# Graph layers on one Trainium2 core: the adjacency for the masks in SBUF in place of PSUM, and seven common PSUM tiles in place of six

## The chip, the core and the metric

The kernel runs on one core of a Trainium2 chip. A core has TensorE (matrix products; PE in the profile, PEld for its weight loads), VectorE (DVE), ScalarE (ACT), GpSimd (POOL) and SyncE (SP, which issues the transfers here), each with an instruction queue of its own. Two on-chip memories matter in this document: SBUF, the working memory, and PSUM, into which TensorE writes its products. The metric is the device time in microseconds (us) of one launch.

## The reference

The input is a batch of 128 graphs of 128 nodes with 256 features each, and one integer adjacency matrix per graph. Two layers follow one another. The first is a graph attention layer: two rounds of attention with a softmax masked by `adj > 0`, a LayerNorm, a feed-forward block with ReLU, a second LayerNorm. The second layer is a transformer layer with eight heads whose attention weights are split by relation. That split is what the change touches:

```python
q = (src @ Wq + bq) ...; k = (src @ Wk + bk) ...          # 8 heads of 32 features
attn = softmax(q k^T / sqrt(dh))
out = 0
for r in range(4):                                        # four relations
    v_r = src @ Wv[r] + bv[r]
    mask = (adj_matrix == r)
    out = out + einsum('bhij,bhjd->bhid', attn * mask, v_r)
x = LayerNorm(src + out @ Wo + bo)
return LayerNorm(x + gelu(x @ W1 + b1) @ W2 + b2)
```

All of it is in 32-bit floats. (The adjacency holds only 0 and 1 here, but all four relations are computed.)

## The kernel before

The graphs are handled in 32 groups of four (`G = 4`). The stages of neighbouring groups (graph attention, first feed-forward, second attention, second feed-forward) are interleaved: a list of times decides in which order the Python code emits the steps of all groups, and TensorE's queue keeps that order. The other engines' queues are ordered when the program is built. Each group takes one turn of a pattern that repeats.

The pools of buffers:

```python
wk = ctx.enter_context(tc.tile_pool(name="wk", bufs=2))                    # SBUF
ps = ctx.enter_context(tc.tile_pool(name="ps", bufs=6, space=PSUM))        # the common tiles "mm"
```

In the second layer's attention, the adjacency of the group is turned from integers to floats once, and then serves 16 products: four graphs by four relations. Each product makes the masked attention weights of all eight heads of one graph (128 x 1024 elements):

```python
adj = ps.tile([P, G, N], F32, name="adj", bufs=1)          # L434
nc.vector.tensor_copy(adj, at)                             # L435, from int32 in SBUF
...
def turned(e):                                             # attention weights, transposed
    eT = wk.tile([P, H, N], F32, name="eT")
    transposed(e, eT, direct, e)                           # VectorE by blocks (L262), then DRAM and back
    return eT

def by_relation(b, eT, ms, parts):
    ab = adj[:, b][:, None, :].to_broadcast([P, H, N])
    for r in parts:
        m = ms[r] = wk.tile([P, H, N], F32, name="m", bufs=R)
        nc.vector.scalar_tensor_tensor(m, ab, r, eT, op0=OP.is_equal, op1=OP.mult)    # L470

def weighted(ms, v):
    po = ps.tile([P, DC, N], F32, name="av", bufs=1)
    ...                                                    # L489: TensorE, 64 products from ms and v
```

The first layer's attention has a similar mask, `cap`, in SBUF:

```python
def gat_weighting(wh, c, cap, direct):
    ...
    nc.vector.scalar_tensor_tensor(e, cap, BIG, e, op0=OP.subtract, op1=OP.min)       # L374
    ...
    nc.gpsimd.tensor_mul(e, e, per_row(s, N))              # L381

def gat_block(direct, tag, g, xt, at):
    cap = wk.tile([P, G, N], F32, name="cap")              # two buffers
    nc.vector.tensor_scalar(cap, at, 0, 2 * BIG, op0=OP.is_gt, op1=OP.mult)           # L387
```

The feed-forward block forms the first product from seven partial products (L307 on TensorE) that are added up partly in PSUM and partly on VectorE. Cut to one unit:

```python
chain, side = (ps.tile([P, 2, T // 2], F32, name="mm") for _ in range(2))
product(chain, 1, True); product(side, 5, True)
nc.scalar.copy(lo[:, :, 0], chain); nc.scalar.copy(hi[:, :, 1], side)
yield
p = ps.tile([P, 2, T // 2], F32, name="mm")
product(chain, 6); product(p, 2, True); product(side, 3)
nc.scalar.copy(lo[:, :, 1], chain)
nc.vector.tensor_add(lo[:, :, 0], lo[:, :, 0], p)          # L321
nc.vector.tensor_add(lo[:, :, 1], lo[:, :, 1], side)       # L322
yield
product(chain, 7)
nc.vector.tensor_add(hi[:, :, 1], hi[:, :, 1], chain)      # L325 reads chain
...
yield
product(chain, 4)                                          # writes chain again
```

The second products are L350, with their sum into the tokens on VectorE at L351. GpSimd works from SBUF to SBUF alone: scale and offset of the LayerNorms (`affine`, L245), the small operations of their statistics (L233 to L237), the division of the softmax (L456 and L381), and the sums of the moving operands (L283 to L286). L239 is the LayerNorm's own scaling on ScalarE, L262 a transposition on VectorE ahead of the trip through DRAM, L478 the bias of the values on VectorE. In the preparation of the weights, L200 to L204 are VectorE operations on weights in SBUF.

Of the kernel before, what the change touches and what calls it, by code (L numbers as in the profile page):

```python
# [12 lines left out]
F32 = mybir.dt.float32  # L13
# [4 lines left out]
PSUM = bass.MemoryType.PSUM  # L18
# [4 lines left out]
P = 128  # L23
G = 4
# [33 lines left out]
def graph_layers(ctx: ExitStack, tc: tile.TileContext, a: dict, out: bass.AP):  # L58
# [10 lines left out]
    NG, N, _, D = x.shape  # L69
# [14 lines left out]
    ld = ctx.enter_context(tc.tile_pool(name="ld", bufs=2))  # L84
    wk = ctx.enter_context(tc.tile_pool(name="wk", bufs=2))
    sm = ctx.enter_context(tc.tile_pool(name="sm", bufs=4))
    ps = ctx.enter_context(tc.tile_pool(name="ps", bufs=6, space=PSUM))
    dr = ctx.enter_context(tc.tile_pool(name="dr", bufs=3, space=bass.MemoryType.DRAM))

    ident = cst.tile([P, P], F32, name="ident")  # L90
# [324 lines left out]
    def attention(y, g, first, direct):  # L415
# [15 lines left out]
            for q in range(2):  # L431
                nc.scalar.activation(kbd[c][:, :, q], p, AF.Identity, scale=own[:, q:q + 1], bias=bk_own[q][:, c:c + 1])

        adj = ps.tile([P, G, N], F32, name="adj", bufs=1)  # L434
        nc.vector.tensor_copy(adj, at)  # L435

        def weights(b):
# [125 lines left out]
    def stage_attention(g):  # L563
        if g == 0:
            folded(wq, bq, "02")
            folded(wkk, bk, "02")
            for q in range(2):
                nc.vector.tensor_scalar(bk_own[q], bk, own[:, q:q + 1], None, op0=OP.mult)
            folded(wv_all, bv, "02", rows=True)
            folded(w1, b1, "11")  # L570
            later["w1"] = weight_sums(w1, "w1")
        x2[g] = yield from attention(x1.pop(g), g, g == 0, g == NG - 1)
# [91 lines left out]
```

## Time and profile before

| what | value |
| --- | --- |
| time, median of 3 | 3208.48 us (3208.29 to 3210.35) |
| span of the profiled launch | 3208.9 us, 55180 instructions |
| TensorE busy | 3124.8 us, 97% |
| VectorE busy | 2019.9 us, 63% |
| ScalarE busy | 1688.2 us, 53% |
| GpSimd busy | 1377.3 us, 43% |
| granted TensorE clock, mean | 0.989 |
| mask products L470 (VectorE) | 512 of 1213 ns, 598.8 us busy |
| affine L245 (GpSimd) | 380 of 128x512, 1276 ns; 256 of 128x256, 738 ns |
| softmax division L456 (GpSimd) | 256 of 1040 ns |
| mask step L374 (VectorE) | 64, 681 to 1192 ns, median 693 |
| cast L435 (VectorE) | 32 of 688 ns |

A share is that of the whole span; what an engine's time is worth is seen only from the waits. In the profile's lists, a line gives the start in us from the span's start, the duration in us, the engine, the line of the kernel, the operation, output and inputs with their shapes, and how often it ran; several like instructions in a row are drawn together. In brackets stands how long the engine sat idle before, and which instruction it waited for. A list of waits gives the engine and line that waited, what released it, and the time in total, how many times, and the longest.

### The profile page before, as it was taken

The numbers are of one execution on the slowest core, as the hardware profiler recorded it, in microseconds if no ns is written. First come the engines' busy times: TensorE is split into PE (matmuls) and PEld (weight loads), VectorE is DVE, ScalarE is ACT, GpSimd is POOL, SyncE is SP. The second block draws the span as 40 slices with busy tenths as digits, with TensorE's granted clock in tenths as the row PEclk, the third lists the DMA queues.
The fourth block names the chain that finished last, engine by engine and source line by source line (L and its number), as shares of the span: only waits on it lengthen the run. The fifth ranks groups of instructions, "written<-read, shape, count | busy, mean of one in ns | idle before, by whom it ended". The sixth has DMA issues, their size and how long they took to land.

```text
span 3208.9 us, 55180 instructions
## 1 busy us (share of the span) xinstructions
PE 3124.8 (97%) x20160; PEld 2377.2 (74%) x20160; DVE 2019.9 (63%) x3654; ACT 1688.2 (53%) x5063; POOL 1377.3 (43%) x1734
## 2 busy tenths in 40 slices
PE   6989999999999999999999999999999999999998
PEld 5756777777777777777777777777777777777666
DVE  3566566666566666576666576666576666576563
ACT  4435555555555555555555555555555555555443
POOL 2324345345345344345344345344345344345342
PEclk8999999999999999999999999999999999999999
DMA  4244454444454444454444454444454444454310
GB/s 156 66 105 96 102 119 102 107 99 100 102 120 104 105 98 101 101 120 104 105 100 98 101 120 104 104 99 99 102 120 104 104 99 99 102 120 92 73 34 14
DMA packets 1156399, 320.82 MB, mean 100 GB/s; under 512 B 902944, under 2 KB 1126688, under 8 KB 1156000
## 3 DMA queue, kind: packets, MB, share of 16 engines
q1 hardware_dynamic: 1156128, 317.29, 43.5%
q8 instruction: 160, 2.62, 0.3%
q14 instruction: 111, 0.91, 0.1%
HBM read 187.58 MB, written 129.62 MB: 99 GB/s over the span
## 4 chain that ended last, share of the span: by engine, by line
PE 58%; DVE 4%; DMA 1%; issue 0%; ACT 0%; POOL 0%; SPq 0%; ACTq 0%; POOLq 0%; DVEq 0%
PE mm L350 18%; PE mm L307 15%; PE mm L477 7%; PE av L489 5%; DVE m L470 3%; PE mm L444 3%; PE mm L527 2%; PE mm L430 2%; PE mm L424 2%; PE mm L392 2%; PE mm L400 1%; PE mm L410 1%; DVE fT L325 0%; DVE fT L322 0%; DMA eT<-zd 0%
## 5 line engine op out<-in xcount | busy, mean ns | idle before, releaser
L470 DVE SCALAR_TENSOR_TENSOR m<-adj,eT 128x1024 f32<-128x1024 f32 x512 | 598.8, 1213 | 242.5 <-DMA eT<-zd 176.9
L245 POOL TENSOR_TENSOR tok<-tok,ln_rows 128x512 f32<-128x512 f32 (+1 forms) x636 | 668.6, 1059 | 42.2 <-PE mm L256 14.8
L456 POOL TENSOR_TENSOR e<-e,s 128x512 f32<-128x512 f32 x256 | 266.1, 1040 | 660.9 <-DVE s L455 648.9
L454 ACT ACTIVATE e<-mm,nm 128x128 f32<-128x128 f32 x1024 | 359.8, 374 | 199.7 <-DVE nm L450 178.0
L477 PE MATMUL mm<-wv,T 128*128 128x512 f32 x1024 | 464.2, 596 | 0.0
L350 PE MATMUL mm<-wf,fT 128*128 128x256 f32 x2048 | 456.9, 381 | 0.0
L350 PE MATMUL mm<-w,fT 128*128 128x256 f32 x2048 | 455.5, 381 | 1.1 <-DVE v L478 1.1
L350 PEld LDWEIGHTS mm<-w,fT 128*128 128x128 f32 x2048 | 386.6, 190 | 75.5 <-issue 23.8
L350 PEld LDWEIGHTS mm<-wf,fT 128*128 128x128 f32 x2048 | 386.4, 190 | 63.3 <-ACT wh L401 8.9
L239 ACT ACTIVATE tok<-tok,nmr,rstd 128x256 f32<-128x256 f32 x512 | 269.2, 594 | 137.7 <-POOL nmr L237 125.1
L477 PEld LDWEIGHTS mm<-wv,T 128*128 128x128 f32 x1024 | 191.5, 190 | 199.6 <-issue 189.3
L351 DVE TENSOR_TENSOR tok<-tok,mm 128x512 f32<-128x512 f32 x128 | 87.8, 686 | 299.4 <-PE mm L350 295.4
L381 POOL TENSOR_TENSOR e<-e,s 128x512 f32<-128x512 f32 x64 | 66.9, 1046 | 475.3 <-DVE s L380 381.1
L489 PE MATMUL av<-m,v 128*32 128x128 f32 x8192 | 256.2, 277 | 8.1 <-DVE v L478 4.2
L489 PEld LDWEIGHTS av<-m,v 128*32 128x32 f32 x8192 | 219.8, 111 | 54.1 <-issue 42.2
L283 POOL TENSOR_TENSOR t<-T 128x256 f32<-128x256 f32 x64 | 46.7, 729 | 483.6 <-DMA T<-zd 483.6
L454 ACT ACTIVATION_READ_ACCUMULATOR e<-mm,nm 128x1 f32 x1024 | 218.8, 214 | 0.0
L450 DVE TENSOR_REDUCE nm<-mm 128x4 f32<-128x512 f32 x256 | 162.9, 676 | 64.0 <-PE mm L444 64.0
L478 DVE TENSOR_TENSOR v<-mm,bv 128x512 f32<-128x512 f32 x256 | 167.5, 684 | 46.9 <-PE mm L477 46.9
L307 PE MATMUL mm<-T,w 128*128 128x256 f32 x768 | 196.5, 385 | 0.2 <-ACT T L260 0.2
L307 PE MATMUL mm<-T,wf 128*128 128x256 f32 x768 | 192.6, 380 | 0.0
L373 ACT ACTIVATE e<-e,wh 128x128 f32<-128x128 f32 x240 | 77.3, 408 | 210.2 <-DMA e<-zsd 210.2
(123 smaller groups left out, 5090.1 us busy)
## 6 DMA issues: line engine op xcount, KB each, us to landing
zd<-e SPq DMA_DIRECT2D x496, 128.0 KB, 3.1
eT<-zd SPq DMA_DIRECT2D x124, 512.0 KB, 4.0
zd<-T SPq DMA_DIRECT2D x364, 128.0 KB, 4.0
T<-zd SPq DMA_DIRECT2D x91, 512.0 KB, 4.0
xt<-in_xT_dram SPq DMA_DIRECT2D x32, 512.0 KB
at<-in_adjT_dram SPq DMA_DIRECT2D x64, 256.0 KB, 6.2
tok<-in_x_dram SPq DMA_DIRECT2D x32, 512.0 KB
out_dram<-tok SPq DMA_DIRECT2D x31, 512.0 KB, 7.5
```

The costliest lines, as they stand in the source:

```text
L239: nc.scalar.activation(y[:, b], y[:, b], AF.Identity, bias=nmr[:, b:b + 1], scale=rstd[:, b:b + 1])
L245: engine.tensor_tensor(y[:, b:b + n], y[:, b:b + n], v[:, None, :].to_broadcast([P, n, D]), op)
L307: nc.tensor.matmul(p[:, i], win[k][:, ts(f0 + i, P)], hs[k], start=first and i == 0, stop=True, skip_group_check=True)
L350: nc.tensor.matmul(p[:, b - b2_], fT[f][:, ts(b, N)], wout[:, f], start=n == 0, stop=n == FC - 1)
L444: nc.tensor.matmul(scores[h][:, c], qT[rows, c, ts(b, N)], kbd[c][rows, b], start=True, stop=True, tile_position=(h * P // 2, 0))
L450: nc.vector.tensor_reduce(nm, p, AX.X, OP.max, negate=True)
L454: nc.scalar.activation(eh[:, q], p[:, q], AF.Exp, bias=nm[:, q:q + 1], accum_out=s[:, q:q + 1])
L456: nc.gpsimd.tensor_mul(eh, eh, per_row(s, N))
L470: nc.vector.scalar_tensor_tensor(m, ab, r, eT, op0=OP.is_equal, op1=OP.mult)
L477: nc.tensor.matmul(p, hT[:, b, f], wv[:, f, r:r + 2], start=f == 0, stop=f == DC - 1)
L478: nc.vector.tensor_add(v[:, r:r + 2].rearrange("p r d -> p (r d)"), p.rearrange("p r d -> p (r d)"), bv[:, r * D:(r + 2) * D])
L489: last = nc.tensor.matmul(po[ts(q, DH), c], v[:, r, c * P + q * DH:c * P + (q + 1) * DH], ms[r][:, q // 2 * HC + c * 2 + q % 2], start=r = ...
```

## The change

The float copy of the adjacency leaves PSUM for SBUF, where it shares the two buffers of `cap`. The tile of PSUM that it leaves free goes to the common pool, which all products use, so that TensorE may be one more tile ahead of the engines that read its results.

```diff
-    ps = ctx.enter_context(tc.tile_pool(name="ps", bufs=6, space=PSUM))
+    ps = ctx.enter_context(tc.tile_pool(name="ps", bufs=7, space=PSUM))
...
-        adj = ps.tile([P, G, N], F32, name="adj", bufs=1)
+        adj = wk.tile([P, G, N], F32, name="adj", tag="cap")
         nc.vector.tensor_copy(adj, at)
```

Nothing else differs: the same instructions with the same shapes run on the same engines.

## The prediction

> **What bounds the kernel now.** I read the page's shares first (TensorE, PE, busy 97% of 3208.9 us; VectorE, DVE, 63%; ScalarE, ACT, 53%; GpSimd, POOL, 43%), then busy time by window, TensorE's waits, the chain that ended last, and the timelines of VectorE and GpSimd. From about 300 to 2880 us the kernel repeats itself: one stall of TensorE comes back at 2052.01 and, five groups later, at 2533.22 us, so a group takes 481.21 / 5 = 96.24 us. One such group:
>
> ```profile
> core 0: us, PE busy (x) PEld busy (x) DVE busy (x) ACT busy (x) POOL busy (x), PEclk, DMA share, GB/s
> 1500.00:1596.20 96.20, 95.63 (x635) 72.93 (x628) 62.48 (x114) 52.60 (x158) 43.23 (x56) 1.00 0.47 106
> ```
>
> TensorE is idle for 0.57 us of it. Its waits, restricted to 300 to 2880 us, are one line, for one reason, once a group:
>
> ```profile
> PE mm L307 <- DVE fT L325: 16.2, 27, 1.1
> ```
>
> The chain of work in that group runs on TensorE everywhere except here, where it passes over VectorE:
>
> ```profile
> 1565.96 0.04 issue
> 1565.99 3.48 DVE m L470 x3
> 1569.47 0.59 DVE fT L322
> 1570.06 0.61 DVE fT L325
> 1570.67 0.14 issue
> 1570.81 1.97 PE mm L307 x8
> ```
>
> Columns are start, duration, what. The reader is to see three mask products (L470), which nobody on TensorE needs at that moment, standing in VectorE's queue ahead of L322 and L325; L325 reads the accumulator that TensorE's next products (L307) will overwrite, so they wait for it. **At this one place in each group VectorE has no slack: what lengthens those masks lengthens the kernel.** The other three sets of masks end 7.9, 9.2 and 12.0 us ahead of the L489 products that read them (masks over at 1509.36, 1536.26, 1583.68; products from 1517.28, 1545.46, 1595.71); the set at this place ends 5.0 us ahead (1569.47 against 1574.44).
>
> **What the Trainium skill says.** "SBUF — State Buffer", section "Who interferes with whom": a VectorE instruction with two SBUF inputs contends with a GpSimd instruction that reads SBUF, while one with at most one SBUF input, outside the two-port modes, does not. The mask product now reads adj from PSUM and eT from SBUF; after the change it reads both from SBUF. The trace agrees on both sides. L470 takes 1190 to 1226 ns in all 512 cases, whatever GpSimd does. L374, the one frequent VectorE product with two SBUF inputs, varies from 681 to 1192 ns:
>
> ```profile
> 1554.24 2.61 POOL L245 TENSOR_TENSOR tok<-tok,ln_rows 128x512 f32<-128x512 f32 x2
> ...
> 1556.22 1.18 DVE L374 SCALAR_TENSOR_TENSOR e<-cap,e 128x512 f32<-128x512 f32 x1
> ...
> 1588.85 0.69 DVE L374 SCALAR_TENSOR_TENSOR e<-cap,e 128x512 f32<-128x512 f32 x1 [4.03 <-ACT e L373]
> ```
>
> The first began 0.63 us ahead of GpSimd's end (1556.85) and took 0.49 us more; the second, with GpSimd idle, took 0.69. Second place, "PSUM — Partial Sum Buffer", section "Specifications (TRN2)": eight banks of 2 KiB per partition. An mm tile, adj (4x128 floats) and av each take one: 6+1+1 before, 7+1 after, both full. Third, "VectorE: DVE Perf Modes", section "Why PSUM operands drop a tier": an fp32 copy with a PSUM operand runs at one element a cycle, SBUF to SBUF at two. The trace agrees: 512 elements from int32 take 688 ns into PSUM (L435) and 412 ns into SBUF (L387). Fourth, "Perfetto Trace Analysis", section "Optimization Strategy" under "Identifying Performance Opportunities": a consistent bubble can mean too few buffers. Here the trace speaks against it: the bubble's releaser is L325, which reads the same accumulator that is written again, and not a tile that would come out of the pool.
>
> **Part by part.** *Seven tiles.* In the steady part nothing waits for a free tile: 0.57 us a group is all there is, and its cause is the dependency above. Matmuls run evenly there (32 products of L350 in 6.91 us of the chain, 216 ns each), so a deeper pool can't speed them either. TensorE's listed waits before 300 us (the largest 5.29 us for POOL L381, 3.92 for masks) and after 2880 us are for data too. I allow -3 us, a choice.
>
> *The cast L435.* 0.69 becomes about 0.41 us, once a group, at a place where TensorE doesn't wait for VectorE: 0.
>
> *The buffer.* adj takes one of the two buffers tagged cap. In a group cap is written at 1521.91 and last read at 1588.85; adj is written at 1536.50, right behind the last mask set of the group before. Two tensors alternate over two buffers, adj having had one all along; all writers and readers are on VectorE, in order. No new wait: 0.
>
> *The masks.* Without contention I leave L470 at 1.21 us: two SBUF inputs cost L374 693 ns in the median, a PSUM and an SBUF input cost L478 684, the same shape. With contention each of the 16 masks of a group pays where a GpSimd read is under way. How the two engines share is seen once in the trace, when weights are prepared around 109 us (between the lines lie others of the two engines):
>
> ```profile
> 108.65 1.24 POOL L245 TENSOR_TENSOR tok<-tok,ln_rows 128x256 f32<-128x256 f32 x1
> ...
> 109.22 1.21 DVE L203 TENSOR_TENSOR w<-w 128x512 f32<-128x512 f32 x1
> ```
>
> A lone 128x256 L245 takes 0.74 us and a VectorE product of 512 elements 0.68; here they take 1.24 and 1.21, each lengthened by about the other's hold, and six L245 stretch over 6.63 us. So they alternate, one instruction each; neither engine is shut out for long. At the place without slack the two queues are:
>
> ```profile
> 1564.10 1.28 POOL L245 TENSOR_TENSOR tok<-tok,ln_rows 128x512 f32<-128x512 f32 x1
> ...
> 1564.86 4.61 DVE L470 SCALAR_TENSOR_TENSOR m<-adj,eT 128x1024 f32<-128x1024 f32 x4
> ...
> 1565.46 0.23 POOL L233 TENSOR_SCALAR rstd<-mv 128x4 f32<-128x4 f32 x1
> 1565.77 0.23 POOL L235 TENSOR_SCALAR nmr<-mv 128x4 f32<-128x4 f32 x1
> 1565.96 0.20 POOL L237 TENSOR_TENSOR nmr<-nmr,rstd 128x4 f32<-128x4 f32 x1
> 1566.11 0.73 POOL L245 TENSOR_TENSOR tok<-tok,ln_rows 128x256 f32<-128x256 f32 x1
> ```
>
> The first mask meets L245 until 1565.38: 0.52 us of overlap, less the 0.14 us that L374's case left free (0.63 - 0.49), is 0.38. With alternation one small operation of 128x4 goes between masks 1 and 2, one between 2 and 3, one between 3 and 4. Each is 0.20 to 0.23 us long[...]; I take 0.1 for each, a choice. Together 0.38 + 0.3 = about 0.7 us, straight onto L325 and TensorE. From 300 to 2880 us there are 27 such places, 30 in the whole list of waits: 30 x 0.7 = **21 us**.
>
> *The other masks.* At 1501.51 the first meets L286, at 1579.95 and 1581.35 they meet L456: 0.5 to 1 us each, on VectorE or on GpSimd, with slacks of 5 us and more: 0 for TensorE. GpSimd loses about 3 us behind the four masks (its L237 at 1565.96 has to let three masks pass), which delays the LayerNorm on ScalarE and the transpose L262 at 1572.37; VectorE then idles 2.20 us before 1575.81 anyway, which takes most of it up.
>
> *Ends.* In the first 300 and the last 330 us TensorE does wait for masks, values and GpSimd (3.92, 1.88, 5.29, 3.29 us at the start; 2.34, 0.85, 2.79 at the end), and longer masks and GpSimd operations land there in part: +6 us, a choice.
>
> Sum: 3208.5 + 21 + 6 - 3 = 3232 us.
>
> **The rivals.** (1) *The contention is hidden.* Then the time stays at 3208, at best a little under it. For it: all averages (VectorE 63%, GpSimd 43%) leave room. Against it: the chain above. (2) *The stall vanishes.* If the order of VectorE's queue comes out differently because the seventh tile or the new costs change the planned order, L325 may come ahead of the masks; 0.57 us x 30 = 17 us would be gained: 3191. Nothing in the profile speaks for or against it, since the order is made when the program is built; TensorE's order is pinned. (3) *GpSimd goes first.* If every waiting GpSimd operation passes ahead of VectorE's next mask, not one each in turn, the four masks pay for nearly all GpSimd work from 1564.86 to 1569.47: about 3.5 us of it reads whole rows; less overheads 2.5 to 3 us a group, 75 to 90 us: about 3290. The head's alternation speaks against it. (4) *VectorE becomes the bound.* With 62.48 us busy a group, all 16 masks delayed by 1 us each would make 78 us of 96: not yet.
>
> **Range and chances.** The middle is the sum, 3232. Rivals 1 and 2 set the low end, 3200; the doubled site cost (1.5 us x 30 = 45) with a second place losing its slack sets the high end, 3275. Faster by over 2% would need 64 us, more than all of TensorE's idle time in the steady part (17 us) and what the ends could yield: 0.01. Slower by over 2% (above 3272.6) is rival 3 or an unlucky order: 0.12. Within 2%: 0.87.
>
> **What would show it.** Right: L470 spread from 1.19 up to about 2.2 us with a mean of 1.35 to 1.6; L245 and L456 longer in the mean; L435 at 0.41; TensorE's wait for L325 up from 0.57 to about 1.3 us a group, and a group of about 97 us. Wrong: L470 still at 1213 ns throughout (no contention), waits for L325 gone (another order), or a new line in TensorE's waits as large as this one (a slack that I called sufficient was not).

## The result and the profile after

The changed kernel takes 3343.48 us (median of 4 runs, 3338.31 to 3349.62) against 3209.41 us for the kernel before (4 runs, 3208.29 to 3210.38): a ratio of 1.0419, 95% interval 1.0395 to 1.0442. It is slower by 134 us; 24 were predicted.

The page after, its busy times and the line of the masks (busy us, then mean ns of one):

```profile
PE 3164.2 (95%) x20160; PEld 2389.9 (72%) x20160; DVE 2128.9 (64%) x3654; ACT 1682.4 (50%) x5063; POOL 1618.9 (49%) x1734
...
L470 DVE SCALAR_TENSOR_TENSOR m<-adj,eT 128x1024 f32<-128x1024 f32 x512 | 717.3, 1438 | 236.4 <-DMA eT<-zd 216.8
```

The reader is to see that both partners of the contention grew: the masks from 1213 to 1438 ns (118 us in all), GpSimd's busy time from 1377.3 to 1618.9 us (242 us), though GpSimd has the same work. One L470 now lasts anything from 1182 to 2310 ns. Neither engine is near its limit, so the averages alone would still allow a kernel of 3209 us. TensorE's waits between 300 and 2880 us don't:

```profile
PE mm L307 <- DVE fT L325: 54.1, 26, 2.4
PE mm L444 <- ACT fT L333: 20.4, 21, 1.1
PE mm L307 <- ACT fT L313: 5.3, 8, 1.6
PE mm L350 <- DVE v L478: 4.5, 8, 1.3
```

Before, only the first of these was there, with 16.2 us. It has more than tripled, and a second wait, for ScalarE, is new. One group of the changed kernel, several engines in one list; lines between those shown are left out, here and in the lists that follow:

```profile
1529.92 5.09 DVE L470 SCALAR_TENSOR_TENSOR m<-adj,eT 128x1024 f32<-128x1024 f32 x3
...
1530.09 3.85 POOL L245 TENSOR_TENSOR tok<-tok,ln_rows 128x512 f32<-128x512 f32 x2
...
1534.02 1.09 POOL L233 TENSOR_SCALAR rstd<-mv 128x4 f32<-128x4 f32 x1
...
1535.62 2.08 ACT L239 ACTIVATE tok<-tok,nmr,rstd 128x256 f32<-128x256 f32 x4 [4.24 <-POOL nmr L237]
1538.09 1.97 PE L307 MATMUL mm<-t,wf 128*128 128x256 f32 x8 [1.87 <-DVE fT L325]
...
1539.77 2.08 ACT L239 ACTIVATE tok<-tok,nmr,rstd 128x256 f32<-128x256 f32 x4 [2.08 <-POOL nmr L237]
1541.75 1.32 ACT L327 ACTIVATE fT<-fT,col 128x512 f32<-128x512 f32 x2
...
1545.44 1.13 PE L444 MATMUL mm<-kbd,T 64*128 64x256 f32 x6 [1.13 <-ACT fT L333]
```

Two things are to be read from it. First, VectorE's queue has another order than before: three masks now stand ahead of the last L321 and a fourth ahead of L322, and beside the three stand two full-width L245. Three masks take 5.09 us (1.70 each, about 1.15 before), two L245 3.85 (1.93 each, 1.28 before). Second, an operation of 128x4 elements, L233, took 1.09 us instead of 0.23. Behind it L237 came late, so ScalarE stood still for 4.24 us, and everything behind L239 in ScalarE's queue, L327 and L333, moved back with it. L333 reads the accumulators that the next products of TensorE overwrite.

Starting each group at the L307 that waits, a group takes 100.24 us in the mean of 26, against 96.27 before. From the starts of each line on TensorE, compared with before, 1.50 us of the 3.97 are lost at L307, 1.33 between L489 and L350 (where L444 waits for L333), 0.35 at other L307 products, where they wait for ScalarE's L313, 0.26 ahead of L350, where it waits for the values L478, and 0.42 in products that last longer, all of them in groups in which the granted clock fell; the last 0.1 is spread. Between 300 and 2880 us it fell to 0.50 seven times, for 3.41 us each, and not once before the change. One of the seven, TensorE alone (start and end, length, busy time and count, granted clock, then the transfers):

```profile
934.88:938.29 3.41, 3.41 (x10) 0.50 0.00 0
```

Added up over the launch: the first such L307 starts 13.5 us later (332.4 against 318.9), 26 groups lose 26 x 3.97 = 103.2, and the end 11.3. Together that is the difference of the two profiled spans, 3337.0 - 3208.9 = 128.1 us.

### The profile page after: what moved, and what is told of

It is laid out like the page before. It is cut to its first block, busy times and chain, and to the rows that moved or that the text cites. A ratio compares the mean times of both kernels' runs of the same rounds, so it can differ in the third digit from the quotient of the medians.

```text
span 3337.0 us, 55148 instructions
## 1 busy us (share of the span) xinstructions
PE 3164.2 (95%) x20160; PEld 2389.9 (72%) x20160; DVE 2128.9 (64%) x3654; ACT 1682.4 (50%) x5063; POOL 1618.9 (49%) x1734
## 5 line engine op out<-in xcount | busy, mean ns | idle before, releaser
L470 DVE SCALAR_TENSOR_TENSOR m<-adj,eT 128x1024 f32<-128x1024 f32 x512 | 717.3, 1438 | 236.4 <-DMA eT<-zd 216.8
L245 POOL TENSOR_TENSOR tok<-tok,ln_rows 128x512 f32<-128x512 f32 (+1 forms) x636 | 737.1, 1168 | 39.0 <-PE mm L256 15.0
L456 POOL TENSOR_TENSOR e<-e,s 128x512 f32<-128x512 f32 x256 | 320.8, 1258 | 624.5 <-DVE s L455 609.9
L350 PE MATMUL mm<-w,fT 128*128 128x256 f32 x2048 | 457.3, 381 | 5.0 <-DVE v L478 4.8
L350 PE MATMUL mm<-wf,fT 128*128 128x256 f32 x2048 | 460.4, 383 | 0.9 <-ACT fT L333 0.9
L350 PEld LDWEIGHTS mm<-w,fT 128*128 128x128 f32 x2048 | 385.3, 190 | 84.4 <-DVE v L478 21.3
L350 PEld LDWEIGHTS mm<-wf,fT 128*128 128x128 f32 x2048 | 388.6, 191 | 65.2 <-ACT wh L401 9.3
L239 ACT ACTIVATE tok<-tok,nmr,rstd 128x256 f32<-128x256 f32 x512 | 265.7, 593 | 270.0 <-POOL nmr L237 258.5
L489 PE MATMUL av<-m,v 128*32 128x128 f32 x8192 | 257.0, 278 | 15.0 <-DVE v L478 10.7
L381 POOL TENSOR_TENSOR e<-e,s 128x512 f32<-128x512 f32 x64 | 67.0, 1046 | 408.6 <-DVE s L380 304.5
L489 PEld LDWEIGHTS av<-m,v 128*32 128x32 f32 x8192 | 220.4, 111 | 60.5 <-issue 41.2
L307 PE MATMUL mm<-T,w 128*128 128x256 f32 x768 | 198.1, 387 | 3.5 <-DVE tok L411 3.2
L307 PE MATMUL mm<-T,wf 128*128 128x256 f32 x768 | 192.6, 380 | 0.0
L444 PE MATMUL mm<-kbd,T 64*128 64x256 f32 x1024 | 162.9, 407 | 20.9 <-ACT fT L333 20.9
L230 DVE BATCH_NORM_STATS2 st<-tok 128x6 f32<-128x256 f32 x512 | 181.1, 409 | 0.5
```

The source lines that it names most:

```text
L230: nc.vector.bn_stats(st, y[:, b])
L239: nc.scalar.activation(y[:, b], y[:, b], AF.Identity, bias=nmr[:, b:b + 1], scale=rstd[:, b:b + 1])
L245: engine.tensor_tensor(y[:, b:b + n], y[:, b:b + n], v[:, None, :].to_broadcast([P, n, D]), op)
L307: nc.tensor.matmul(p[:, i], win[k][:, ts(f0 + i, P)], hs[k], start=first and i == 0, stop=True, skip_group_check=True)
L350: nc.tensor.matmul(p[:, b - b2_], fT[f][:, ts(b, N)], wout[:, f], start=n == 0, stop=n == FC - 1)
L444: nc.tensor.matmul(scores[h][:, c], qT[rows, c, ts(b, N)], kbd[c][rows, b], start=True, stop=True, tile_position=(h * P // 2, 0))
```

## The experiments

**How they are built.** The theory is that adj in SBUF makes masks and GpSimd block one another, and that the loss comes through the waits above. The first rival: the seventh tile led to another planned order of the queues, and the order costs the time. In runs marked "order held", an order recorded from the kernel before (from the changed one in one_input) is imposed on all engines by ordering dependencies between neighbours in a queue. This puts 64 lines ahead of the code, so in their profiles every line number is higher by 64: L371 is L307, L389 L325, L397 L333, L303 L239, L309 L245, L414 L350, L464 L400, L508 L444, L534 L470, L542 L478, L553 L489, L591 L527. Ratios are to the kernel before, with 95% intervals.

### Contention or order: five runs

**six_tiles.** The changed kernel with the common pool as before. Its queues come out in the order of the kernel before, with nothing imposed (VectorE's differs in 36 of 3659 places, near the end).

```diff
-    ps = ctx.enter_context(tc.tile_pool(name="ps", bufs=7, space=PSUM))
+    ps = ctx.enter_context(tc.tile_pool(name="ps", bufs=6, space=PSUM))
```

> Adjacency in SBUF, but six common tiles (one bank of PSUM stays empty). Built so, PE, ACT, GpSimd and SP have their queues in the order of before, and VectorE's differs in 36 of 3659 places. Theory C (the masks' two SBUF inputs collide with GpSimd, and this alone costs the 134 us): about 3340 us, L470 with a mean of 1.40 us or more. Theory O (the seventh tile changes the planned order of the queues, and the new order is what costs; contention costs only what I predicted for it): 3225 to 3245 us. If the two only act together: in between.

Measured: 3354.55 us, 1.0447 (1.0431 to 1.0463). adj in SBUF alone, in the old order, costs all of it and slightly more. Since the order is the old one, this trace can be laid beside the site shown in the prediction:

```profile
1524.80 5.03 DVE L470 SCALAR_TENSOR_TENSOR m<-adj,eT 128x1024 f32<-128x1024 f32 x4
...
1525.42 1.09 POOL L233 TENSOR_SCALAR rstd<-mv 128x4 f32<-128x4 f32 x1
1526.59 1.05 POOL L235 TENSOR_SCALAR nmr<-mv 128x4 f32<-128x4 f32 x1
1527.61 1.14 POOL L237 TENSOR_TENSOR nmr<-nmr,rstd 128x4 f32<-128x4 f32 x1
...
1528.78 2.07 ACT L239 ACTIVATE tok<-tok,nmr,rstd 128x256 f32<-128x256 f32 x4 [3.44 <-POOL nmr L237]
...
1531.16 1.97 PE L307 MATMUL mm<-t,wf 128*128 128x256 f32 x8 [0.99 <-DVE fT L325]
...
1538.35 1.54 ACT L333 ACTIVATE fT<-mm,col 128x256 f32<-128x256 f32 x4
1539.21 1.87 PE L444 MATMUL mm<-kbd,T 64*128 64x256 f32 x8 [2.46 <-ACT fT L333]
```

The four masks take 5.03 us, only 0.42 more than before, and TensorE's wait for L325 grows by the same 0.42, from 0.57 to 0.99. Each small GpSimd operation, however, waits for one whole mask: 1.09, 1.05 and 1.14 us instead of 0.23, 0.23 and 0.20. The first L237 ends 3.95 us after the masks began, against 1.30 before; the second 8.71 against 5.07. So the second block of L239 is 3.6 us late relative to the masks, L327 and L333 behind it as well, and TensorE waits 2.46 us at L444, where it hadn't waited at all. L327 needed L325's sums, which had been there since 1531.62; it started at 1535.52, when L239 was through. The Trainium skill, "TensorE: Matmul & The Clock Gate", section "Architectural detail: the array is 16× 32×32, not 1× 128×128", states that ScalarE's and VectorE's queues are strictly first in, first out; these times agree.

The wait at L444 has a second cost. Windows of the same trace, TensorE alone:

```profile
1336.11:1339.52 3.41, 1.68 (x8) 1.00 0.84 131
1339.52:1342.93 3.41, 3.41 (x9) 0.50 0.36 83
...
1537.49:1540.91 3.42, 1.67 (x8) 1.00 0.84 131
1540.91:1544.32 3.41, 3.41 (x9) 0.50 0.34 74
1544.32:1547.73 3.41, 3.41 (x18) 1.00 0.76 262
```

From 1540.91 us, 1.7 us after the wait, which ended at 1539.21, the granted clock is 0.50 for 3.41 us, and 32 products of L350 take 8.79 us in place of 7.17. About every second group shows it: groups last 101.5 and 99.9 us in turn. The same page of the skill, section "What's actually happening" under its Part 1, states that the clock falls to half after an idle window of about 3.4 us and that the windows run freely. The half rate agrees. The idle time does not: here a wait of 2.46 us was enough, in a stretch of 3.42 us in which TensorE was still busy for 1.67, and the measurement decides. The free running fits: the two low stretches shown begin 201.39 us apart, which is 59 times 3.413 us, and that is also the time of two groups. So in every second group the wait lies in the same place of such a window.

**after_old_order.** Both parts of the change, order held.

```diff
     ps = ... bufs=7 ...; adj = wk.tile(..., tag="cap")
+    # all queues held in the order of the kernel before
```

> The changed kernel (seven tiles, adjacency in SBUF) with all five queues held in the order of before. Theory C: about 3340 us. Theory O: 3225 to 3245 us, and the same as with six tiles, as nothing waited for a free tile in the steady part. A gain of the seventh tile by itself would show as a difference from the six-tile kernel.

Measured: 3366.61 us, 1.0502 (1.0466 to 1.0539). With the old order held the full change is no faster, so its new order isn't what makes it slow. The extra tile shortens the single wait at L444 (46.8 us in 26 waits, 63.9 in six_tiles), but the low clock follows in nearly every group:

```profile
837.65:844.47 6.82, 6.67 (x17) 0.50 0.67 151
...
940.05:946.87 6.82, 6.67 (x17) 0.50 0.69 154
...
1042.45:1049.27 6.82, 6.70 (x17) 0.50 0.46 87
```

These begin 102.40 us apart, 30 times 3.413 us, and that is the time of one such group: each meets the window as the one before did. The mean granted clock of the launch is 0.967 (0.981 in six_tiles, 0.985 in the changed kernel).

**av_common.** Seven common tiles with adj still in PSUM; the tile that this takes is won from the weighted sums instead, which now come from the common pool. VectorE's order becomes nearly that of the changed kernel.

```diff
-        adj = wk.tile([P, G, N], F32, name="adj", tag="cap")
+        adj = ps.tile([P, G, N], F32, name="adj", bufs=1)
...
-            po = ps.tile([P, DC, N], F32, name="av", bufs=1)
+            po = ps.tile([P, DC, N], F32, name="mm")
```

> Seven common tiles with the adjacency left in PSUM: the accumulator av takes its tile from the common pool, which frees a bank. No mask has two SBUF inputs. VectorE's queue is then nearly that of the changed kernel (120 of 3659 places differ from it, 771 from before). Theory C: 3195 to 3215 us, L470 at 1.21 us throughout. Theory O: 3300 us or more, with masks standing between L321, L322 and L325 and a value sum L478 behind the four masks that wait for a transfer.

Measured: 3238.79 us, 1.0092 (1.0076 to 1.0107). All 512 masks take 1185 to 1226 ns. Seven tiles and nearly the new order without contention cost 29 us, over the 3195 to 3215 us expected, of which the shared tile for the sums may have a part: not a pure measurement of the order.

**one_input** and **one_input_old.** Seven tiles; each mask product is replaced by a transposition of eT, of the same shape and with one input in SBUF. The relations are left out of the result, and adj is computed but not read. The first has the changed kernel's order exactly, the second the old one; both orders are held.

```diff
-                nc.vector.scalar_tensor_tensor(m, ab, r, eT, op0=OP.is_equal, op1=OP.mult)
+                nc.vector.transpose(m, eT)
```

> The changed kernel with all queues held exactly in its own order, and each mask product replaced by a block transposition of eT of the same size (128x1024): one SBUF input, no masking, so the relations are left out of the result. The transposition of this size takes 1.23 us where it occurs before. Theory C: about 3210 us, no stretched GpSimd operations. Theory O: still 3300 us or more, as the order is the same. In between: what is left above 3210 is the order's share.

> Seven tiles, masks replaced by block transpositions of the same size (one SBUF input, relations left out), all queues in the order of before. What the new order costs by itself is the difference from the same kernel with the new order (3222 us): if the order costs the 13 us that stood above before, this is 3205 to 3212 us; if the transposition is what costs them, 3220 us.

Measured: 3222.22 us, 1.0038 (1.0024 to 1.0053), and 3208.52 us, 0.9993 (0.9984 to 1.0001). With one SBUF input in place of the masks' two the loss is all but gone, with seven tiles and in either order, and so is the stretching on GpSimd: in one_input every L233 of 128x4 takes 232 to 246 ns, as before (up to 1157 in the changed kernel). Two results follow: contention is the cause of about nine tenths of the loss, and the new order by itself costs 3222.22 - 3208.52 = 13.7 us. The latter lies at the start: one_input's groups are as long as before (96.32 us), but the first of them starts 12.4 us later than in one_input_old, behind this wait, which one_input_old doesn't have:

```profile
248.13 3.45 PE L553 MATMUL av<-m,v 128*32 128x128 f32 x64 [8.64 <-DVE v L542]
```

The changed kernel has it too (7.82 us at 251.24). In the first 200 us TensorE's own order differs too, in 234 places; the prediction took it for pinned, which holds in the steady part only. And the seventh tile alone gains nothing that can be measured without contention: one_input_old equals the kernel before. With contention and the old order it comes out 12 us slower (3366.61 against 3354.55 us), with the lowered clock in more groups.

### Where the contention hurts: seven runs

The theory after six_tiles: late statistics on GpSimd delay L239, and with it L333, because all stand in one queue. If so, moving one of the three engines' instructions must shift the wait. All seven have the order held but for the moves shown; each is made in 28 groups, and xN is a number of instructions. Where nothing else is said there are six common tiles and adj is in SBUF.

**scale_later.**

```diff
 ScalarE
-  L327 x2, L239 x8,           L327 x2, L333 x8
+  L327 x2, L239 x4,           L327 x2, L333 x8, L239 x4
```

> The six-tile kernel with the adjacency in SBUF and all queues in the order of before, but for one move in each group on ScalarE: the four scalings L239 of the second of two LayerNorms in a row stand behind L327 and L333 in place of ahead of them. Theory S (the masks hold GpSimd's small operations L233, L235, L237 up, L237 comes late, L239 blocks ScalarE's queue in front of L333, and L333 is what frees the accumulators that TensorE needs for L444 and L350): the wait of L444 for L333, 2.46 us a group, goes, and with it the lowered clock behind it; about 3215 to 3235 us. Theory M (the masks' own length ahead of L325 is what costs): no change, about 3350 us.

Measured: 3359.21 us, 1.0462 (1.0448 to 1.0477). The gain expected under theory S did not come. L444's wait for L333 is gone, which shows that the place of L239 in the queue caused it; but new waits came (its waits between 300 and 2880 us):

```profile
PE mm L591 <- DVE v L542: 45.7, 25, 2.8
PE av L553 <- DVE v L542: 26.7, 26, 2.2
```

As read from the trace, the later half of L239 delays the transposition of the tokens, its trip through DRAM and a row of scores behind it in the transfer queue; VectorE stands still 6.09 us for these scores, and the values (L542, that is L478) behind them are late. That half of L239 is urgent as well. The lateness must be taken away where it arises.

**two_first.** The kernel before (adj in PSUM), with VectorE's order changed so that two of the four masks let the chain pass. This takes the known 0.57 us wait away.

```diff
 VectorE
-  L470 x4, L322, L325 x2,          L478 x2
+  L470 x2, L322, L325 x2, L470 x2, L478 x2
```

> The kernel before (adjacency in PSUM, six tiles) with the move on VectorE alone: in each group two of the four masks stand behind L322 and L325. If the 0.57 us that TensorE waits for L325 is that queue and nothing else, it vanishes: 28 groups at 0.57 to 0.74 us are 16 to 21 us, so 3188 to 3194 us. If another wait takes its place: 3209.

Measured: 3210.29 us, 0.9999 (0.9991 to 1.0007). The wait for L325 is gone and the time is the same. The list of weight loads, for 28 groups, shows where it went:

```profile
PEld mm L508 <- ACT fT L397: 20.9, 56, 0.4
```

That is 0.75 us a group, at L444 behind ScalarE's L333: **already before the change, two chains ended within about 0.1 us of one another, and the wait at the first hid the second.** TensorE's list of waits showed only the first.

**both_moves.** scale_later and two_first's move together, with adj in SBUF.

```diff
 ScalarE as in scale_later, VectorE as in two_first
```

> As scale_later, and on VectorE two of the four masks of the zero-slack place stand behind L322 and L325 in place of ahead of them. Under theory S the time is that of scale_later less the wait of L307 for L325 (0.99 us a group with six tiles): 3190 to 3215 us, though all masks still have two SBUF inputs. Under theory M: at least 25 us less than scale_later, but still over 3300.

Measured: 3329.41 us, 1.0369 (1.0355 to 1.0383): 30 us better than scale_later. The waits for L542 ahead of L591 (45.4 us) remain, beside 26.9 us of L307 for ScalarE's L313 and 18.6 of L400 for L333.

**six_stats_first.** GpSimd computes both sets of statistics before the affines that stood between them.

```diff
 GpSimd
-  L381, L233, L235, L245, L236, L245, L233, L235, L237, L245, L236, L245 x2, L237
+  L381, L233, L235, L236, L237, L233, L235, L236, L237, L245 x5
```

> Six tiles, adjacency in SBUF, all queues in the order of before but for GpSimd's: in each group the statistics of two LayerNorms (L233, L235, L236, L237, twice) stand ahead of five affine operations L245 in place of among them, and so mostly ahead of the four masks. Theory S2 (the masks make GpSimd's L237 late by about 3 us, and this reaches TensorE over L239, either through L333 and the accumulators or through the transposition L262 and the transfers behind it): 3215 to 3250 us, with no wait for L333 over 0.5 us a group. Rival D (VectorE and GpSimd can't do their common work one after the other in the time of a group, whatever their order): still 3320 us or more.

Measured: 3311.15 us, 1.0311 (1.0292 to 1.0329), 43 us better than six_tiles. The wait at L444 is gone, as it must be if the statistics delay it. But the other one grew, from 0.99 to 2.74 us:

```profile
1511.22 6.78 DVE L534 SCALAR_TENSOR_TENSOR m<-adj,eT 128x1024 f32<-128x1024 f32 x4
...
1512.45 12.12 POOL L309 TENSOR_TENSOR tok<-tok,ln_rows 128x512 f32<-128x512 f32 x8
...
1519.34 1.97 PE L371 MATMUL mm<-t,wf 128*128 128x256 f32 x8 [2.74 <-DVE fT L389]
```

Beside the masks there is now an unbroken row of wide affines. The two engines take turns instruction by instruction here, so now the masks pay in full: 6.78 us for four, where 128x4 operations between them had made it 5.03. The loss is moved from GpSimd's chain to VectorE's, which stands on the same TensorE.

**six_stats_two.** The same, with the VectorE move of two_first.

```diff
 GpSimd as in six_stats_first, VectorE as in two_first
```

> As six_stats_first, and two of the four masks stand behind L322 and L325 on VectorE. Under S2 the wait for L325 goes too: 3190 to 3225 us with all masks from SBUF. Under D: over 3300.

Measured: 3260.64 us, 1.0147 (1.013 to 1.0164), 94 of six_tiles' 145 us recovered. Both waits at this place are gone but for one of 1.0 us, and a third has come: behind the two masks that were moved, the values L478 are late for L400. TensorE's waits between 300 and 2880 us (L464 is L400, L377 L313):

```profile
PE mm L591 <- DVE v L542: 14.5, 22, 2.4
PE mm L464 <- DVE v L542: 11.6, 27, 2.4
PE mm L371 <- ACT fT L377: 10.8, 6, 1.8
```

The largest lies at the mask set of another graph:

```profile
1526.71 3.20 DVE L534 SCALAR_TENSOR_TENSOR m<-adj,eT 128x1024 f32<-128x1024 f32 x2 [0.63 <-DMA eT<-zd]
...
1528.79 1.71 POOL L349 TENSOR_TENSOR T<-T 128x256 f32<-128x256 f32 x1
...
1533.52 0.67 PE L591 MATMUL mm<-wo,oT 128*128 128x256 f32 x2 [1.17 <-DVE v L542]
```

Two masks last 3.20 us beside the sums of moving operands (L349 is L285: 1.71 us, 0.73 before), and the values L542 behind them are late for L591. These links are read from the trace; no run took them away.

**after_stats_first.** GpSimd's move with seven tiles.

```diff
 bufs=7, adj in SBUF; GpSimd as in six_stats_first
```

> The changed kernel (seven tiles, adjacency in SBUF) with the queues in the order of before and GpSimd's statistics first. Under S2: 3215 to 3250 us, within 10 us of the six-tile one; a gain of the seventh tile would show as the difference. Under D: 3320 us or more.

Measured: 3304.27 us, 1.0298 (1.0282 to 1.0314), 62 us better than after_old_order. It agrees with six_stats_first.

**before_stats_two.** Both moves in the kernel before, adj in PSUM.

```diff
 bufs=6, adj in PSUM; GpSimd as in six_stats_first, VectorE as in two_first
```

> The kernel before (adjacency in PSUM, six tiles) with both moves. The earlier run with the VectorE move alone changed nothing, because the wait for L325 became one of 0.7 us for L333, behind L239 and L237. If L237 is what that wait comes from, both are gone: 28 groups at 0.74 us are 21 us, so 3186 to 3194 us. If a third wait of the same size lies behind: 3209.

Measured: 3186.43 us, 0.9927 (0.9914 to 0.9939): **faster than both kernels**, and 24 us ahead of the one before (3210.51 us on the same chip). Its list of TensorE's waits in the steady part is empty and a group takes 95.43 us. two_first's move alone gave nothing; together with the earlier statistics it does, which confirms the second chain. The same eight affines that took 12.12 us in six_stats_first run undisturbed here:

```profile
1556.82 9.32 POOL L309 TENSOR_TENSOR tok<-tok,ln_rows 128x512 f32<-128x512 f32 x8
```

**What the seven runs show together.** With adj in SBUF none of the five came down to what theory S or S2 expected. scale_later and both_moves came out where rival M had put them (about 3350 us, then at least 25 less but over 3300); 3311, 3304 and 3261 us lie between S2 and rival D. The waits went where each move should send them, so the path over L237, L239 and L333 is real; but it is one of several that are about equally tight, and clearing one brings out the next. What contention costs can't be put down to one path.

## Why the prediction was wrong

**The mechanism was right.** adj in SBUF made the masks contend with GpSimd; L470's mean (1438 ns) and the cast L435 (0.42 us) are in the ranges given; the engines alternate one instruction each in the places shown, as read from the head of the launch, and GpSimd doesn't shut VectorE out (rival 3). (One affine near the end had to let three masks pass and took 4.51 us.) VectorE didn't become the bound (rival 4): 66.41 of 101.16 us in a group. The contention was not hidden (rival 1).

**The term at L325** was 0.7 us a group. In the predicted order it was 0.42 (six_tiles): the right order of size, somewhat high. In the changed kernel it was 1.50, because its queues were planned differently and set wide affines beside the masks; that it equals the 1.5 us of the prediction's worst case is luck: that figure was the 0.7 doubled, and not worked out for this order. The small 128x4 operations were entered at 0.1 us each for the masks; what they cost was on GpSimd's side, a whole mask each. Rival 2 reckoned with another order only as a gain; an unlucky one was named among the chances, without a cost. After one_input and one_input_old the order costs 13.7 us without contention; with it, the changed kernel is 23 us faster than after_old_order. Neither is a large part of the 134.

**The step that failed** is this one: "GpSimd loses about 3 us behind the four masks (its L237 at 1565.96 has to let three masks pass), which delays the LayerNorm on ScalarE and the transpose L262 at 1572.37; VectorE then idles 2.20 us before 1575.81 anyway, which takes most of it up". The size was right: 2.65 and 3.64 us in six_tiles. The consequence was not. It followed the delay from ScalarE to VectorE alone and found slack there. It didn't ask what else stands in ScalarE's queue behind L239: L327 and L333, which free TensorE's accumulators. That path was as tight as the one through L325, which two_first shows, and the view on which "TensorE's waits are one line, for one reason" rested couldn't show it: once TensorE has waited for the first chain, the second one isn't late any more. So a term put at 0 was 3.30 us a group at L444 in six_tiles (2.53 ahead of its first product, 0.77 up to L350), with 0.86 us behind it in L350 at the lower clock, and 1.33 us in the changed kernel. The prediction had named this sign of being wrong: a new line in TensorE's waits. Over its 26 groups the changed kernel lost 39 us at L325, where 21 were predicted, 35 at L444 and 16 at two further waits, where 0 was, and 11 to the lower clock, which the prediction left out.

**The small terms.** The two further waits, 0.61 us a group in the changed kernel, are of the same kinds. Slacks measured from masks to the products that read them said nothing of the values L478 queued behind the masks (0.26); and L313 stands in ScalarE's queue behind another L239 (0.35), which at 1172.69 us had waited 1.30 us for L237. The ends, +6, were 13.5 at the start, most of it the new order, and 11.3 at the end. The seventh tile, -3, is 0 by one_input_old. The range ended at 3275 because its worst case had 45 us for the site at L325 and about 18 for a second one, and no third.

**What stays open**: what exactly lowers the clock. The distances of 201.39 and 102.40 us fit its falling in every second group of one run and in nearly every group of the other; they don't say what counts within a window: in after_old_order TensorE was busy for 1.64 us of the 3.42 from 1237.01 us, no more than in the two stretches shown of six_tiles, and the clock stayed at 1.00. Open too are the 50 us that six_stats_two still lacks, for which only the reading above is given, and whether any order of the queues would win all of it back.

## What to carry to other kernels

When an operand moves into the memory that another engine is reading, list for every instruction of both engines what it will have to let pass, and follow each delayed result into every queue in which it stands, in order, down to the instruction that frees a buffer of the bounding engine. Short operations on a chain suffered most here: each paid a whole mask of the other side. A list with one single wait doesn't mean one tight chain; take that wait away (here by moving two masks) and see whether the time moves.

## What the hardware showed that was not expected

- Beside masks of 1.2 us with two SBUF inputs, GpSimd's L233, L235 and L237 of 128x4 elements took 1.05 to 1.14 us instead of 0.20 to 0.23. The price was about that of one mask, however little the operation itself had to do.
- A wait of TensorE of 2.46 us was enough for a granted clock of 0.50 that began 1.7 us after its end and lasted 3.41 us. In the steady part of the changed kernel, six_tiles and after_old_order such stretches lasted 3.41 or 6.83 us, and they began whole multiples of 3.413 us apart; a group that is itself such a multiple (102.40 us in after_old_order) fell into the low clock at the same place each time.
